# Five small edits to a hybrid scan, attention and mixture-of-experts kernel: where block 0's weights are copied, when choices are counted, and how a sigmoid is made

## The chip, the cores and the metric

The kernel runs on one core of a Trainium2 chip. The metric is the device time of one execution in microseconds (us), as the median of several runs. The engines are TensorE (PE, matmuls), VectorE (DVE), ScalarE (ACT, activation functions and copies), GpSimd (POOL) and SyncE (SP, which only starts transfers). Each engine works through its own queue of instructions in order, and semaphores make one wait for another.

## What is computed

The input is 8 sequences of 512 tokens with 256 features. Four residual blocks follow one another, each on a layernorm of its input:

```python
x = x + scan_block(layernorm(x))     # silu(x @ Win), a linear recurrence over tokens, @ Wout
x = x + mixture(layernorm(x))        # routed and shared experts
x = x + attention(layernorm(x))      # 16 heads of 16, causal, scores clipped to +-10
x = x + mixture(layernorm(x))        # the same weights again
```

The mixture is the part that the edits touch most:

```python
scores = sigmoid(x @ router_w.T)                  # 16 experts
s = scores + bias
# the best 2 of 4 groups of experts, by the sum of each group's two highest s
# then the 4 highest s within these groups
tw = 2.5 * scores[chosen] / (scores[chosen].sum() + 1e-20)
routed = sum over chosen e of tw[e] * ((silu(x @ gate[e]) * (x @ up[e])) @ down[e])
shared = (silu(x @ sh_gate) * (x @ sh_up)) @ sh_down
```

Everything is float32.

## The kernel before, in words

The work has four stages. In the profiled execution they lie at about 0 to 359 us (scan), 359 to 765 (first routed experts), 765 to 1331 (attention) and 1331 to 1758 (second routed experts and the final sums).

**The two stretches.** `stretch(layer)` (L1236) runs the scan and later the attention, one sequence ("batch", b = 0 to 7) after the other. Beside each batch's main work it carries the routing of the batch before it, the shared experts of the batch before that, and the layernorm and transposes of a batch to come. Each of these is a generator of steps, and `timed(...)` gives each step a fraction of the main work at which it is issued. The written order is then what a scheduler starts from; it may reorder instructions on each engine by its own estimates, except where `tc.issue_after` ties one behind another or `keep_in_program_order` pins it.

**Routing one batch.** `Route` (L550) normalises, transposes (`turned`, L385; `pt_m`, copies at L399), and forms logits (`pl_m`, L590). ACT turns them into `score_m` by the sigmoid of L599. A chain of some thirty VectorE operations in `choices` (L602) finds the four experts and writes `sel_m` (L649). TensorE then counts: two small matmuls `pr_m` (L656, L657) give each choice its place among all choices of its expert. VectorE makes `row_m`, `where_m`, `slots_m` from that, and GpSimd scatters the rows to memory (L706) so that each expert's rows lie together. The last batches, 6 and 7, have tighter fractions (L1329 to L1332), since the routed stage can start only when all are counted.

**Attention.** For each of four groups of heads: scores `ps_a` (L1096), exponentials on ACT (L1107) into `w_all` or `es_a`, clamping on VectorE (L1110, L1118), products with the values `po_a` (L1131), a copy `oT_a` on ACT (L1144), transposes `pto_a` (L1147), and the division by the row sums (`rec_a`, `o_a`, L1149, L1150). Then `pt_oa` and the output projection `py_a` (L454). The exponential and the sigmoid are in different tables of ACT, so ACT loads a table (ACT_TABLE_LOAD) when it goes from one to the other. The shared experts of this stretch use tanh (L972), and those of the scan use sigmoid (L976).

**Shared experts.** `shared_experts` (L943): `pg_m` matmuls of 512 columns (L958), `pd_m` matmuls (L987), a copy `ys_m` (L995). The list `wide` always holds the `pg_m` matmul made last.

**Routed experts.** `routed(i)` (L806) works on blocks of 128 sorted rows. 136 blocks are always run; an `If` (L939) holds further ones that this input does not need, so each routed stage begins behind a branch that all engines take. For block n: `load` (L833) reads the rows from memory and, for every fourth block, reads four table entries to registers (L816); `fetch` (L846) copies the block's gate weights by ACT and its up weights by VectorE from the big weight tile `w_all` to small tiles; `turn` (L854) transposes the rows on PE (`pt`, L858) and ACT copies them back (L859); `up` (L861) has 16 matmuls `ph` (L869), the sigmoid (L877) and two products; `down` (L893) has the matmuls `pyr` (L897), a scaling on ACT (L905) and an adding scatter on GpSimd (L906). Fetches run one block ahead of `up` in the written order.

**Buffers.** The small weight tiles, most routing temporaries and the scan's `xi_s` and `state_s` share one tag, "col", of 6 buffers; the scan's `y_s` and the transposed activations share "kb4", of 9. The residual stream `x` has a pool of 3 buffers of its own, `xpool`.

**The start.** `first_two` (L1277) brings batches 0 and 1 of the scan up together: layernorm of batch 0, its transposes `pt_l` with two copies to `xT_l` (L399), the input projection `pz_s` (L500), layernorm of batch 1 pinned on VectorE, the scans (L509 to L516). `layer.copies` says which engines make the two copies of a transpose: in the scan `by_scalar` (both ACT), in the attention `by_both` (ACT and VectorE).

Of the kernel before, what the change touches and what calls it, by code (L numbers as in the profile page):

```python
# [15 lines left out]
P = 128  # L16
# [58 lines left out]
def tile_hybrid_block(  # L75
# [280 lines left out]
    def timed(steps, *places):  # L356


        def scaled():
            now = 0  # L360
            for place in places:
                yield place - now
                now = place
                next(steps)
            for _ in steps:
                pass

        return Piece(1, scaled())
# [4 lines left out]
    def some(steps, many: int):  # L373

        for _ in range(many):
            yield next(steps)

    def issue(piece):
        for _ in piece.steps:
            pass  # L380
# [204 lines left out]
    def logits(i: int, b: int, tag: str, held):  # L585
        xnT = held["xnT"]
        pl = bank([P, NT, E], f"pl_{tag}")
        for t in range(NT):
            for k in range(KD):
                nc.tensor.matmul(  # L590
                    pl[:, t, :],
                    lhsT=xnT[:, k, t * P : (t + 1) * P],
                    rhs=rw_sb[:, k, :],
                    start=(k == 0),
                    stop=(k == KD - 1),
                )
            yield
        score = small.tile([P, NT, E], FP, tag="score", name=f"score_{tag}")
        nc.scalar.activation(score, pl, AF.Sigmoid)  # L599
        held["score"] = score  # L600

    def choices(i: int, b: int, tag: str, held, paced: bool):  # L602
# [50 lines left out]

        pr = bank([P, 2, NT, E], f"pr_{tag}")
        flat = sel.rearrange("p t e -> p (t e)")
        nc.tensor.matmul(pr[:, 0].rearrange("p t e -> p (t e)"), lhsT=tri, rhs=flat, start=True, stop=True)  # L656
        nc.tensor.matmul(pr[:, 1].rearrange("p t e -> p (t e)"), lhsT=ones, rhs=flat, start=True, stop=True)  # L657
        row = small.tile([P, NT + 1, E], FP, tag="row", name=f"row_{tag}", bufs=3)
        nc.vector.tensor_copy(row[:, 0, :], counts[i])
        for t in range(NT):  # L660
# [145 lines left out]
    def routed(i: int, table, beside):  # L806
# [39 lines left out]
        def fetch(n: int):  # L846


            for half, (copy, name) in enumerate(((nc.scalar.copy, "gate"), (nc.vector.tensor_copy, "up"))):
                here = work.tile([P, KD * F], FP, tag="col", name=f"{name}_{i}_{n}", bufs=COLS)  # L850
                copy(here, w_all[:, bass.ds(held[n][0] + half * KD * F, KD * F)])  # L851
                held[n].append(here)

# [382 lines left out]
    def stretch(layer):  # L1236


        i = layer.mixture
        xT, xn, made, routes, sends = {}, {}, {}, {}, []  # L1240

        def norm(b: int, first: bool = False):
            def place():
                xn[b] = kb4(f"xn_{i}_{b}")
                return xn[b]

            return normed(b, f"l{i}_{b}", place, first, first)

        def turn(b: int, copies=layer.copies):
            return turned(lambda: xn.pop(b), f"l{i}_{b}", lambda xnT: xT.update({b: xnT}), copies)  # L1250

        def project(b: int):
            made[b], piece = layer.project(b, xT.pop(b))
            return piece

        def store(b: int):
            nc.sync.dma_start(out=rows_of(parts[i][0], b), in_=x_tiles[b])

        def experts(b: int):
            return shared_experts(i, b, lambda: routes.pop(b).held["xnT"], i == 1)  # L1260

        for b in range(layer.ahead):
            if b < layer.early:
                if b in unturned:
                    issue(Piece(0, unturned.pop(b)))
                xT[b] = ready.pop(b)
            else:
                layer.load(b)
                first = i == 0 and b == 0
                issue(Piece(0, norm(b, first)))  # L1270
                issue(Piece(0, turn(b)))
                if first:
                    load_shared()
            if b == 0:
                issue(project(b))

        def first_two():  # L1277

            layer.load(1)
            issue(Piece(0, norm(1, True)))  # L1280
            for _ in range(2):
                pending.pop(0)()
            main = layer.main(0, made.pop(0))
            issue(Piece(0, some(main.steps, NI)))
            issue(Piece(0, turn(1)))
            issue(project(1))
            second = layer.main(1, made.pop(1))
            issue(Piece(0, some(second.steps, NI)))
            issue(main)
            return Piece(second.columns - NI * KD * T, second.steps)  # L1290

        def start_route(b: int):
            routes[b] = Route(i, b, layer.copies)
            store(b)
            return routes[b]

        begun = None
        if layer.mixture == 0:
            begun = first_two()
        for b in range(1 if begun else 0, B):  # L1300
            pieces = [begun or layer.main(b, made.pop(b))]
            begun = None
            nxt, last = b + layer.ahead, b == B - 1
            fill = []
            if layer.ahead > 1 and not last:
                fill.append(project(b + 1))
            if b > 1:
                shared_sum = experts(b - 2)
                if last:

                    each = shared_sum.columns // 12
                    rest = Piece((12 - HELD) * each, shared_sum.steps)

                    many = HELD * each if layer.mixture else HELD * each * 3 // 2
                    shared_sum = Piece(many, some(shared_sum.steps, HELD))
                fill.append(shared_sum)
                pieces.append(timed(sends.pop(), 0.1, 0.14, 0.18, *spread(0.22, 0.66 if last else 0.86, NT * TK)))
            if fill:
                pieces.append(behind(*fill))
            if b > 0:  # L1320
                r = start_route(b - 1)
                if last:
                    pieces.append(timed(r.norm(), *spread(0.0, 0.12, NT), *spread(*layer.last_rows, NT)))
                else:
                    first, then, rows, full = layer.norms
                    pieces.append(timed(r.norm(), *spread(first, then, NT), *spread(rows, full, NT)))
                sends.append(r.rest)
                if last:
                    pieces += [  # L1329
                        timed(r.scores(), *layer.last_scores, *spread(0.5, 0.56, NT)),  # L1330
                        timed(some(r.rest, PICKS), *spread(0.57, 0.7, PICKS)),
                        timed(some(r.rest, 3 + SENT), 0.72, 0.74, 0.76, *spread(0.78, 1.0, SENT)),  # L1332
                    ]
                else:
                    pieces += [
                        timed(r.scores(), *layer.scores[:2], *spread(*layer.scores[2:], NT)),
                        timed(some(r.rest, PICKS), *spread(*layer.choose, PICKS)),
                    ]
            if nxt < B:
                added = layer.load(nxt)  # L1340
                if added is not None:
                    pieces.append(timed(added, 0.24, 0.28))
                pieces += [
                    timed(norm(nxt), *spread(0.32, 0.44, NT), *spread(0.56, 0.64, NT)),
                    timed(turn(nxt), 0.75, 0.79),
                ]
            issue(beside(*pieces))
            if layer.ahead == 1 and nxt < B:
                issue(project(nxt))
            if i == 0 and b == 2:  # L1350
                for make in pending:
                    make()
        layer.end()

        r = start_route(B - 1)
        chain = 3 + PICKS
        issue(
            beside(  # L1360
                behind(rest, experts(B - 2)),
                timed(r.norm(by_vector=True), *spread(0.0, 0.05, 2 * NT)),
                timed(sends.pop(), *spread(0.0, 0.5, NT * TK - SENT)),
                timed(r.scores(), 0.2, 0.22, *spread(0.28, 0.33, NT)),
                timed(some(r.rest, chain + 8), *spread(0.36, 0.68, chain), *spread(0.7, 1.0, 8)),
            )
        )
        table = []
        issue(
            beside(  # L1370
                experts(B - 1),
                timed(r.rest, *spread(0.0, 0.5, NT * TK - 8)),
                timed(blocks(i, table), 0.03, 0.14, 0.26, 0.38),
            )
        )
        return table
# [140 lines left out]
```

## Time and profile before

| | |
|---|---|
| median of 3 runs | 1783.7 us (1783.02 to 1783.77) |
| the profiled execution's own time | 1759.74 us |
| its span, first to last instruction | 1758.0 us |
| PE busy | 1675.9 us, 95% |
| VectorE busy | 1100.0 us, 63% |
| ACT busy | 806.7 us, 46% |
| GpSimd busy | 769.8 us, 44% |
| mean granted TensorE clock | 0.981 of full speed |
| table loads on ACT | 17 of 1283 ns: 1 at L241, 8 at L599, 8 at L1107 |
| period of batches 2 to 5 of the attention | 69.0 us |

The profile is of one execution. A line of its list of groups or of its timeline names the engine, the line of the code, the operation, what it writes and reads, and how often; in brackets stand the idle time of the engine just before and what ended it. The ends of matmuls are modelled. TensorE's clock is granted in windows of 3.41 us, at full speed or at half.

### The profile page before, as it was taken

Reading aid. Unit: us, or ns where it says so; the run is one execution under the profiler, and the core shown is the slowest. Engines: PE = TensorE matmul, PEld = TensorE weight load, DVE = VectorE, ACT = ScalarE, POOL = GpSimd, SP = SyncE. Lnnn points to the kernel's source line nnn. Section 1 sums busy time; section 2 is a strip of 40 time slices with the busy share of each in tenths; the row PEclk is TensorE's granted clock in tenths of the full one; section 3 lists DMA queues with packets and bytes.
Section 4 is the critical chain, followed back from the end, with each engine's and each line's share of the span. In section 5 each row is a group of like instructions: output and inputs, shape, how many; then the busy total and the mean of one; then the engine's idle time right before and its main releaser. Section 6 shows DMA issues by size and latency. Waiting matters only on the chain. (4 is left out here: it accounts for less than half of the span.)

```text
span 1758.0 us, 32867 instructions
## 1 busy us (share of the span) xinstructions
PE 1675.9 (95%) x10640; PEld 1252.9 (71%) x10640; DVE 1100.0 (63%) x3428; ACT 806.7 (46%) x1740; POOL 769.8 (44%) x674
## 2 busy tenths in 40 slices
PE   6899998999999999999999999999999999999993
PEld 3566665589999999944545545545468999999993
DVE  8878877445556655556776576666653655565562
ACT  3222322145555555545654464454423555555551
POOL 3355555535555655420032331322552555455663
PEclk9999999999999999989999999999999999999997
DMA  5444323445555655531012111122543555666666
GB/s 157 139 166 161 133 91 120 163 90 94 98 94 105 108 96 97 103 63 37 25 39 70 68 61 63 52 74 68 184 148 80 98 96 94 111 128 139 119 125 170
DMA packets 149279, 181.38 MB, mean 103 GB/s; under 512 B 16144, under 2 KB 135984, under 8 KB 149104
## 3 DMA queue, kind: packets, MB, share of 16 engines
q0 software_dynamic: 54720, 82.57, 25.0%
q1 hardware_dynamic: 92576, 92.71, 17.6%
q10 hardware_dynamic: 1808, 3.93, 0.6%
q8 instruction: 89, 1.46, 0.3%
q14 instruction: 86, 0.70, 0.1%
HBM read 81.62 MB, written 97.53 MB: 102 GB/s over the span
## 5 line engine op out<-in xcount | busy, mean ns | idle before, releaser
L906 POOL DMA_INDIRECT part<-rows x272 | 426.6, 1568 | 336.8 <-ACT rows L905 244.7
L706 POOL DMA_INDIRECT xg<-sorted_m,slots_m x256 | 256.4, 1002 | 289.5 <-ACT slots_m L703 98.9
L869 PEld LDWEIGHTS ph<-rows,gate 128*128 128x128 f32 x2176 | 285.4, 192 | 21.3 <-ACT rows L859 6.7
L869 PE MATMUL ph<-rows,gate 128*128 128x128 f32 x2176 | 289.4, 276 | 5.1 <-ACT rows L859 5.1
L869 PE MATMUL ph<-rows,up 128*128 128x128 f32 x2176 | 288.7, 276 | 0.0
L897 PE MATMUL pyr<-w_all,rows 128*128 x1088 | 280.5, 380 | 0.9 <-DVE rstd_l L428 0.9
L869 PEld LDWEIGHTS ph<-rows,up 128*128 128x128 f32 x2176 | 266.2, 193 | 0.0
L877 ACT ACTIVATE rows<-ph 128x256 f32<-128x256 f32 x272 | 104.5, 384 | 329.0 <-PE ph L869 329.0
L878 DVE TENSOR_TENSOR rows<-ph,rows 128x256 f32<-128x256 f32 x272 | 115.3, 424 | 193.7 <-ACT rows L877 193.0
L897 PEld LDWEIGHTS pyr<-w_all,rows 128*128 128x128 f32 x1088 | 185.2, 191 | 15.2 <-ACT rows L905 1.3
L851 ACT COPY gate<-w_all 128x512 f32 x272 | 170.0, 626 | 15.2 <-PE ph L869 2.4
L1107 ACT ACTIVATE w_all<-ps_a 128x1024 f32<-128x1024 f32 x128 | 124.4, 1021 | 82.6 <-PE ps_a L1096 77.5
L851 DVE COPY up<-w_all 128x512 f32 x272 | 119.4, 439 | 31.7 <-PE ph L869 17.1
L905 ACT ACTIVATE rows<-pyr,gain 128x256 f32<-128x256 f32 x272 | 128.6, 473 | 15.3 <-PE pyr L897 13.7
L1096 PE MATMUL ps_a<-w_all 32*128 32x512 f32 (+3 forms) x1024 | 123.3, 477 | 7.5 <-ACT w_all L1107 6.4
L958 PE MATMUL pg_m<-xT_m,sg_sb 128*128 128x512 f32 x256 | 124.8, 610 | 0.0
L882 DVE SCALAR_TENSOR_TENSOR gain<-rows,expert_b 128x4 f32<-128x4 f32 x272 | 61.1, 225 | 100.2 <-ACT rows L905 83.5
L958 PE MATMUL pg_m<-xT_m,su_sb 128*128 128x512 f32 x256 | 123.4, 604 | 0.0
L879 DVE TENSOR_TENSOR rows<-ph,rows 128x256 f32<-128x256 f32 x272 | 115.2, 423 | 8.3
L987 PE MATMUL pd_m<-sd_sb,act_m 128*128 128x256 f32 x512 | 119.8, 382 | 0.0
L987 PEld LDWEIGHTS pd_m<-sd_sb,act_m 128*128 128x128 f32 x512 | 95.5, 190 | 20.9 <-issue 4.7
L858 PE MATMUL pt<-ident,rows 128*128 128x128 f32 x544 | 103.7, 273 | 2.9 <-PEq L816 1.0
(219 smaller groups left out, 2215.5 us busy)
## 6 DMA issues: line engine op xcount, KB each, us to landing
rows<-xg SPq DMA_DIRECT2D x272, 136.0 KB, 2.6
part<-x SPq DMA_DIRECT2D x16, 512.0 KB, 3.0
part<-ys_m SPq DMA_DIRECT2D x14, 512.0 KB, 3.0
w_all<-in_L_ffn_gate_w_dram SPq DMA_DIRECT2D x24, 256.0 KB, 5.2
w_all<-in_L_ffn_up_w_dram SPq DMA_DIRECT2D x24, 256.0 KB, 5.8
w_all<-in_L_ffn_down_w_dram SPq DMA_DIRECT2D x24, 256.0 KB, 5.7
sum<-part POOLq DMA_DIRECT2D x10, 512.0 KB, 4.0
xg<-zeros SPq DMA_DIRECT2D x34, 136.0 KB, 2.2
```

The costliest lines, as they stand in the source:

```text
L706: nc.gpsimd.indirect_dma_start(out=xg[i], out_offset=bass.IndirectOffsetOnAxis(ap=slots[:, at : at + 1], axis=0), in_=rows[:, t, :], in_of ...
L851: copy(here, w_all[:, bass.ds(held[n][0] + half * KD * F, KD * F)])
L869: nc.tensor.matmul(ph[:, s, f * P : (f + 1) * P], lhsT=both[s][:, k * F + f * P : k * F + (f + 1) * P], rhs=rows[:, ROW + k * P : ROW + (k ...
L878: nc.vector.tensor_mul(act, ph[:, 0, :], act)
L879: nc.vector.tensor_mul(act, ph[:, 1, :], act)
L897: nc.tensor.matmul(py, lhsT=act[:, f * P : (f + 1) * P], rhs=w_all[:, bass.ds(w + 2 * KD * F + f * D, D)], start=(f == 0), stop=(f == KF - 1),
L905: nc.scalar.mul(rows[:, 0:D], py, gain[:, TK : TK + 1])
L906: nc.gpsimd.indirect_dma_start(out=parts[i][n % 2], out_offset=bass.IndirectOffsetOnAxis(ap=rows[:, D + 2 * TK : D + 2 * TK + 1].bitcast(U ...
L958: made = nc.tensor.matmul(dst, lhsT=w[:, k, f * P : (f + 1) * P], rhs=xnT[:, k, :], start=(k == 0), stop=(k == KD - 1),)
L987: nc.tensor.matmul(py[:, j, :], lhsT=acts[n][:, f, t * P : (t + 1) * P], rhs=shared[n][3][:, f, :], start=(n == 0 and f == 0), stop=(n == ...
L1096: nc.tensor.matmul(ps[j // 2][:, j % 2, col : col + n], lhsT=k_sb[w][r, o, c * P : (c + 1) * P], rhs=q_sb[r, o, c * P : T], start=True, st ...
L1107: nc.scalar.activation(es[two], ps[two][:, :, 0:cols], AF.Exp, scale=ATT_SCALE)
```

## The change

There are five edits.

1. The router's score in the second mixture (the one beside the attention) is made by exp(-x) on ACT, then on VectorE min with 3e38, plus 1, and a reciprocal. The first mixture keeps the sigmoid.
2. In batch 6 of both stretches the two counting matmuls `pr_m` are tied behind the `pg_m` matmul that was issued last.
3. In each routed stage block 0's gate and up are both copied by VectorE, into the two halves of one tile `both` from `xpool`, instead of by ACT and VectorE into two "col" tiles.
4. The first transpose of the scan (batch 0) is copied by ACT and VectorE, instead of twice by ACT.
5. In the last batch of each stretch, the last step of the choices and the sends of the batch before it stand at later fractions.

```diff
--- before.py
+++ after.py
@@ -596,7 +596,13 @@
                 )
             yield
         score = small.tile([P, NT, E], FP, tag="score", name=f"score_{tag}")
-        nc.scalar.activation(score, pl, AF.Sigmoid)
+        if i == 0:
+            nc.scalar.activation(score, pl, AF.Sigmoid)
+        else:
+
+            nc.scalar.activation(score, pl, AF.Exp, scale=-1.0)
+            nc.vector.tensor_scalar(score, score, 3.0e38, 1.0, ALU.min, ALU.add)
+            nc.vector.reciprocal(score, score)
         held["score"] = score
 
     def choices(i: int, b: int, tag: str, held, paced: bool):
@@ -653,8 +659,9 @@
 
         pr = bank([P, 2, NT, E], f"pr_{tag}")
         flat = sel.rearrange("p t e -> p (t e)")
-        nc.tensor.matmul(pr[:, 0].rearrange("p t e -> p (t e)"), lhsT=tri, rhs=flat, start=True, stop=True)
-        nc.tensor.matmul(pr[:, 1].rearrange("p t e -> p (t e)"), lhsT=ones, rhs=flat, start=True, stop=True)
+        with tc.issue_after(wide[-1].ins) if b == B - 2 else nullcontext():
+            nc.tensor.matmul(pr[:, 0].rearrange("p t e -> p (t e)"), lhsT=tri, rhs=flat, start=True, stop=True)
+            nc.tensor.matmul(pr[:, 1].rearrange("p t e -> p (t e)"), lhsT=ones, rhs=flat, start=True, stop=True)
         row = small.tile([P, NT + 1, E], FP, tag="row", name=f"row_{tag}", bufs=3)
         nc.vector.tensor_copy(row[:, 0, :], counts[i])
         for t in range(NT):
@@ -846,8 +853,15 @@
         def fetch(n: int):
 
 
+            if n == 0:
+
+                both = xpool.tile([P, NT, D], FP, tag="x", name=f"both_{i}").rearrange("p t d -> p (t d)")
             for half, (copy, name) in enumerate(((nc.scalar.copy, "gate"), (nc.vector.tensor_copy, "up"))):
-                here = work.tile([P, KD * F], FP, tag="col", name=f"{name}_{i}_{n}", bufs=COLS)
+                if n == 0:
+                    here = both[:, half * KD * F : (half + 1) * KD * F]
+                    copy = nc.vector.tensor_copy
+                else:
+                    here = work.tile([P, KD * F], FP, tag="col", name=f"{name}_{i}_{n}", bufs=COLS)
                 copy(here, w_all[:, bass.ds(held[n][0] + half * KD * F, KD * F)])
                 held[n].append(here)
 
@@ -1268,7 +1282,7 @@
                 layer.load(b)
                 first = i == 0 and b == 0
                 issue(Piece(0, norm(b, first)))
-                issue(Piece(0, turn(b)))
+                issue(Piece(0, turn(b, by_both if first else layer.copies)))
                 if first:
                     load_shared()
             if b == 0:
@@ -1328,8 +1342,8 @@
                 if last:
                     pieces += [
                         timed(r.scores(), *layer.last_scores, *spread(0.5, 0.56, NT)),
-                        timed(some(r.rest, PICKS), *spread(0.57, 0.7, PICKS)),
-                        timed(some(r.rest, 3 + SENT), 0.72, 0.74, 0.76, *spread(0.78, 1.0, SENT)),
+                        timed(some(r.rest, PICKS), *spread(0.57, 0.67, PICKS - 1), 0.76),
+                        timed(some(r.rest, 3 + SENT), 0.79, 0.81, 0.83, *spread(0.85, 1.0, SENT)),
                     ]
                 else:
                     pieces += [
```

In the built order of instructions, edit 3 puts the two VectorE copies of block 0, and the first register loads of L816 on PE, ACT and VectorE, ahead of the branch at L939. Edit 1 leaves four executed table loads: at L241, one at the first L1107, and past the branch of the second routed stage one at L851, before block 1's gate copy, and one at L877, before block 0's sigmoid. Edits 2 and 5 change no order in the first stretch. In the second, batch 6's `pr_m` moves behind `pto_a` and the 24 `po_a` matmuls that read `w_all`, ahead of the eight that read `es_a`; on VectorE the clamps of the last two `es_a` come ahead of `sel_m`, and `rec_a` and `o_a` of the third group directly after it. Edit 4 moves VectorE's half of the copy ahead of the layernorm of batch 1; the first scan operations then stand between that layernorm's steps, and on ACT the `xT_l` copies of batch 1 come after an activation `xi_s` that takes over an earlier `xi_s` buffer, free only once `y_s` has been made from it.

## The prediction

> **What bounds the kernel now.** I read the summary of busy times first, then a table of busy time by stage, then the waits of TensorE (PE), then the timeline around each long one.
>
> ```profile
> PE 1675.9 (95%) x10640; PEld 1252.9 (71%) x10640; DVE 1100.0 (63%) x3428; ACT 806.7 (46%) x1740; POOL 769.8 (44%) x674
> ```
>
> PE is busy 95% of the span of 1758.0 us. So only PE's gaps, and windows in which its clock is halved, can be won or lost. The table by stage (stretch, its length, PE busy, VectorE, ScalarE, GpSimd, granted clock):
>
> ```profile
> 1050.00:1119.00 69.00, 68.92 (x432) 35.38 (x428) 46.03 (x145) 34.55 (x57) 19.84 (x21) 1.00 0.18 64
> 1240.00:1290.00 50.00, 45.77 (x267) 27.46 (x260) 33.72 (x126) 19.16 (x39) 26.02 (x27) 0.97 0.51 171
> ```
>
> The first is one ordinary batch of the attention: PE is full, although ScalarE (ACT) makes two table loads in it. The second holds batch 6, the place that the edits aim at: 4.2 us of PE are idle. The list of PE's waits says for what:
>
> ```profile
> PE pr_m L656 <- DVE sel_m L649: 7.1, 3, 3.2
> PE pz_s L500 <- ACT xT_l L399: 7.0, 1, 7.0
> PE ps_a L1096 <- ACT w_all L1107: 6.4, 13, 1.0
> PE ph L869 <- ACT rows L859: 5.1, 4, 2.3
> ```
>
> These are the three counting waits (batch 6 twice, batch 7 once), one at the start, the small ones on exponentials, and the first blocks of the two routed stages. The timeline of batch 6 and of the second routed stage's start:
>
> ```profile
> 1248.77 1.28 ACT L599 ACT_TABLE_LOAD   x1
> 1250.39 1.28 ACT L1107 ACT_TABLE_LOAD   x1
> ...
> 1257.93 0.43 PE L656 MATMUL pr_m<-sel_m,tri 128*128 128x64 f32 x2 [2.99 <-DVE sel_m L649]
> 1258.50 1.06 PE L1147 MATMUL pto_a<-ident,oT_a 128*128 128x128 f32 x4
> 1263.10 1.98 PE L958 MATMUL pg_m<-xT_m,su_sb 128*128 128x512 f32 x4
> 1266.58 0.30 PE L397 MATMUL pt_oa<-ident,o_a 128*128 128x128 f32 x1 [0.62 <-DVE o_a L1150]
> ...
> 1332.19 1.66 ACT L851 COPY gate<-w_all 128x512 f32 x3 [1.22 <-DMA rows<-xg]
> 1333.76 0.64 ACT L859 COPY rows<-pt 128x256 f32<-128x256 f32 x2
> 1334.17 2.07 PE L869 MATMUL ph<-rows,gate 128*128 128x128 f32 x8 [2.24 <-ACT rows L859]
> ```
>
> Batch 6 stalls 2.99 us for sel_m, and the four transposes after it take 1.06 us where four take 0.60 later: the clock record at 1258.34 is a 3.41 us window at half speed. At the second boundary PE waits 2.24 us while ACT copies three gates of 0.52 us ahead of block 0's rows.
>
> **What the Trainium skill says.** "TensorE: Matmul & The Clock Gate", Part 1, What's actually happening: an idle window of 3413 ns halves the clock, and windows run free of the kernel. The trace agrees in length and speed (every slow record is 3.41 us or a multiple at 0.5), and in freedom: a 3.2 us stall at 292.7 brought two slow windows, the similar idle at 359 to 362 none. "ScalarE: Activation LUTs", What ACT_TABLE_LOAD costs, has 1283 ns and a drain of about 1380 ns. All 17 loads here take 1283 ns; no drain shows: after the load at 1282.71 the activation starts at 1284.00. I take 1.28. "ScalarE activation tables: per-element evaluation and per-set limits", Table sets in the compiler and the runtime, says that loads are placed per block. That fits what the built order of the changed kernel shows: past the branch into the second routed stage ACT has two new loads, one before block 1's gate copy, one before block 0's sigmoid.
>
> **The change, part by part**, against the profiled execution (span 1758.0, time 1759.74). The shown median, 1783.7, is 24.0 longer; I carry differences over unchanged.
>
> *Sigmoid from exp in the second mixture.* It removes 15 loads (all at the scores, and seven of eight at L1107) and adds the two named: net 13 x 1.283 = 16.7 us of ACT. Against that PE gains little. In batches 2 to 5 PE has 68.92 of 69.00: 0, hidden by PE's own matmuls, and with that cover gone it would be worth the 2.6 us per batch. In batch 1 two waits of 0.38 and 0.21 follow the loads at 851.2 and 853.3: -0.6. Two VectorE operations on 128x64 come per batch: no row has these exact ones; between 128x64 operations at 0.23 and a 128x16 reciprocal at 0.26, I take 0.45 for both, bounded by 0.3 and 0.7. They lie in VectorE's slack (46 of 69) except in batch 7, where pr_m already waits 0.87 on sel_m at 1293.30: the load's absence gives back 0.2 there (the last logits end at 1283.76, the score starts at 1284.00), so +0.25.
>
> *Counting later, batch 6.* In the first mixture PE's order is unchanged: 0, and the 3.21 us stall with its two slow windows stays. In the second, pr_m now stands behind the four transposes pto_a and 24 of the 32 po_a matmuls, ahead of the last eight. On VectorE the two pairs of es clamps go ahead of sel_m. Replay: without loads the score is there before VectorE ends its clamps at 1249.6; plus 0.35 s_m starts at 1249.95 (now 1250.32). From s_m to the end of sel_m now takes 7.48 (to 1257.80, next start); with the es clamps, 1.07 (1257.80 to 1258.87), sel_m ends at 1258.5. PE: the ps_a group at 1252.79 takes 0.64 instead of 1.52, because its exponentials come 2.6 earlier; po_a 0.57, so 1254.0. oT is copied from 1254.3 to 1254.9, pto_a ends at 1255.4, 24 po_a at full clock (about 2.1) at 1257.5. A stall of 1.1 remains. Then pr 0.57, po_a 0.55: pg_m starts at 1259.7 instead of 1263.10, pto_a ends at 1262.0. What is late next is o_a, since the row, found and choices operations wait behind the later pr_m: from 1259.2 they need 2.3, then sig 0.6, rec 0.3, act 0.7, o_a ends at 1263.6, and pt_oa follows at 1263.7 against 1266.58: -2.9. A slow window in the remaining stall would give back up to 1.7 (half of 3.41). I take -2.5; bounds -6 (stall, slow window and ps_a waits, all gone: 2.99+0.38+1.7+0.9) and -0.8.
>
> *Block 0's gate and up by VectorE.* The two copies and the register load of the table (L816) move ahead of the branch; VectorE idles 7 us there, so they are hidden, and without it they would cost about 1.1. After the branch ACT still has three gate copies (blocks 1, 2, 3) before rows_0, so the 1.66 us stay; the register load of 0.31 and 0.07 of register work leave: -0.4 at each boundary. At the second the new load stands ahead of the gates: +1.28. The load at the sigmoid falls in ACT's 3.59 us of idle: 0. Blocks 1 to 13 are reordered slightly on each engine; the stages show 401.5 of 405 and 245.5 of 246 us PE busy: 0, within 0.5.
>
> *The first turn by ACT and VectorE.* The second half of xT is copied by VectorE (0.69), ahead of norm(1), and the first scan operations come between. ACT's xT copies of batch 1, on which PE waits 6.95 us to 28.80, now stand behind an activation that waits until y_s has been made and a buffer is free: about 28.6 instead of 28.18. +0.4; bounds -1.0 (batch 0 starts 0.3 earlier, and the clock with it) and +2.5 (norm(1) late by 2.2).
>
> *Later fractions.* No queue but batch 6's changes: 0. GpSimd's order moves one memset, SyncE's queue nothing, so no DMA is issued later: 0.
>
> Sum: -0.6 + 0.25 - 2.5 - 0.4 - 0.4 + 1.28 + 0.4 = -2.0. Time 1757.7 profiled, 1781.7 median.
>
> **The rivals.**
> (a) The counting stall goes wholly, with its slow window, and a window at a boundary is lost as well: -6 + 0.5, or to -8 with a window less. For it: the remaining stall is only 1.1, which VectorE's pipelining may cover. Against: VectorE's queue before sel_m is longer. About 1777.8.
> (b) Slower: the new table load at the second boundary. There PE already idles 0.92 and 2.24 us and meets two slow windows; 0.9 net more idle shifts everything, and the first boundary, with no slow window today, can get one or two by mere phase. One window costs up to 1.7; it decides when two more are met, 3.4, plus 0.9 and a start at its bound of +2.5, against -2.5: +4, 1788. The start's slow windows at 26 and 50 speak for it; that the windows' place is chance speaks against a large chance.
> (c) The loads are on the path after all: -16.7, 1767. Against it is PE's 68.92 of 69.00.
> (d) The moves cancel: the later o_a eats batch 6's gain: 0 to +3, 1785.
>
> **How the numbers follow.** A measurement of this kernel tells about 0.2%, 3.6 us, from no change. The worked case has 0.44, a tenth of all beyond -3.6; (a) 0.28, (b) 0.19, (c) 0.02, (d) 0.07. Faster: 0.10 + 0.28 + 0.02 = 0.40; same: 0.34 + 0.07 = 0.41; slower 0.19. The range runs from 1776.3, where (a) is mostly in, to 1787.8, where most of (b) is; outside are about 0.06 below and 0.12 above. The worked case alone spans 1779 to 1783.5.
>
> **What would show it.** Right: loads fall from 17 to 4; ordinary batches stay 69.0; pr_m in batch 6 waits about 1.1 us, and the next pg_m starts about 3.4 us sooner counted from the batch's pl_m; at the second boundary ph waits about 3.1 us, with a load among the gates; at the first about 1.9; pz_s of batch 1 starts near 29. Wrong: batches below 68.5 us (c); pr_m's wait gone and the clock whole (a); more half-speed windows before 1700 us than the twelve of now, or pz_s after 31 (b). The forecast fails most easily on slow windows, which no order of instructions tells.

## The result and the profile after

The changed kernel takes 1776.7 us (median of 20 runs, 1768.6 to 1781.5), the kernel before in the same comparison 1783.8 (20 runs, 1778.3 to 1789.2). The ratio is 0.9951, with a 95% interval from 0.9938 to 0.9963: 7 us less by the medians, 9 by the ratio, where 2.0 were forecast. The median lies just inside the range given (its lower end is 1776.3); by the ratio the time would be 1775.0, just outside, and the change is about four times the size forecast.

The profile shown for before is of an execution of 1759.74 us, 24 below the median, with a span of 1758.0; that of after is of an ordinary run, with a span of 1777.8. Set side by side, the two say "20 us slower". So the first thing to find out was what the 24 us are.

From the page of after, its first line and TensorE's busy time:

```profile
span 1777.8 us, 32866 instructions
PE 1686.0 (95%) x10640; PEld 1258.2 (71%) x10640; DVE 1100.0 (62%) x3447; ACT 787.9 (44%) x1724; POOL 770.7 (43%) x674
```

ScalarE is busy for 787.9 us instead of 806.7: 13 of the 17 table loads are gone. The stages table shows what that bought in an ordinary batch of the attention (stretch, its length, PE, weight loads, VectorE, ScalarE, GpSimd, clock, share and GB/s of the DMAs; the prediction's tables have the same columns, and its list of them leaves out the weight loads):

```profile
1056.00:1125.00 69.00, 68.91 (x432) 35.39 (x428) 46.58 (x148) 31.97 (x54) 20.00 (x20) 1.00 0.19 64
```

Nothing: 68.91 of 69.0 us, as before, with 2.6 us less on ScalarE. The waits of PE in after, from the third row on (the work that waits and what releases it, then the sum in us, the number and the longest; the lines of after are numbered up to 14 higher):

```profile
PE ph L883 <- ACT rows L873: 5.8, 4, 3.1
PE pg_m L972 <- ACT expert_b L793: 5.1, 1, 5.1
PE ps_a L1110 <- ACT w_all L1121: 5.0, 10, 1.0
PE pr_m L663 <- DVE mv_m L413: 5.0, 1, 5.0
PE pr_m L663 <- DVE sel_m L655: 4.5, 1, 4.5
PE pz_s L500 <- ACT xT_l L399: 2.6, 1, 2.6
```

Two waits of about 5 us and one of 4.5 are new beside the profile shown of before (the 5.0 is the scan's batch 6, which had 3.2; the 4.5 its batch 7). At the start pz_s waits 2.6 us instead of 7.0, but most of that has only moved: the transposes pt_l there now wait four times instead of once, 12.7 us instead of 9.8. The attention's batch 6 is no longer in the list. The second boundary, in the timeline of after:

```profile
1346.89 0.66 PE L872 MATMUL pt<-ident,rows 128*128 128x128 f32 x4 [0.92 <-ACTq L953]
1347.42 1.28 ACT L865 ACT_TABLE_LOAD   x1 [0.83 <-DVE gain L896]
1348.71 1.66 ACT L865 COPY gate<-w_all 128x512 f32 x3
1350.69 3.78 PE L883 MATMUL ph<-rows,both 128*128 128x128 f32 x16 [3.15 <-ACT rows L873]
1350.93 1.28 ACT L891 ACT_TABLE_LOAD   x1
```

The new load stands ahead of the gates and PE waits 3.15 us instead of 2.24; the second load is hidden. That is as forecast.

### The profile page after: what moved, and what is told of

Its sections match the earlier page's. It is cut to its first block, busy times and chain, and to the rows that moved or that the text cites. A ratio compares the mean times of both kernels' runs of the same rounds, so it can differ in the third digit from the quotient of the medians.

```text
span 1777.8 us, 32866 instructions
## 1 busy us (share of the span) xinstructions
PE 1686.0 (95%) x10640; PEld 1258.2 (71%) x10640; DVE 1100.0 (62%) x3447; ACT 787.9 (44%) x1724; POOL 770.7 (43%) x674
## 5 line engine op out<-in xcount | busy, mean ns | idle before, releaser
L972 PE MATMUL pg_m<-xT_m,su_sb 128*128 128x512 f32 x256 | 127.8, 622 | 5.1 <-ACT expert_b L793 5.1
```

Of the source, the lines that this page charges most:

```text
L972: made = nc.tensor.matmul(dst, lhsT=w[:, k, f * P : (f + 1) * P], rhs=xnT[:, k, :], start=(k == 0), stop=(k == KD - 1),)
```

## The experiments

Each study ran on one chip, with the kernel before among its runs. Ratios are to that kernel, with 95% intervals. Two kinds of trace turned up, and all kernels of a study were of one kind: in one kind (the profile shown of before) the kernel before takes about 1762 us, in the other 1784 to 1795. The result above and the first, third and last studies are of the second kind, here called "late"; the other two are "prompt". The exp score, alone or with all five edits, was run only where signals are late.

| kernel | kind | ratio to before |
|---|---|---|
| the kernel before, unchanged | late | 1.0000 (0.9988 to 1.0011) |
| all five edits | late | 0.9964 (0.9952 to 0.9977), again 0.9949 (0.9925 to 0.9972) |
| score only | late | 1.0008 (0.9993 to 1.0022) |
| all but the score | late | 0.9936 (0.9917 to 0.9955), again 0.9945 (0.9927 to 0.9964) |
| first copy only | prompt | 0.9992 (0.9979 to 1.0005) |
| first copy only | late | 0.9947 (0.9922 to 0.9972) |
| later counting only | prompt | 0.9966 (0.9947 to 0.9985) |
| later counting only | late | 0.9982 (0.9964 to 1.0000) |
| block 0's copies only | prompt | 0.9990 (0.9978 to 1.0001) |
| start shifted | prompt | 0.9996 (0.9983 to 1.0009), again 1.0003 (0.9988 to 1.0018) |
| first copy, start shifted | prompt | 1.0002 (0.9990 to 1.0015) |
| first copy, start shifted | late | 1.0003 (0.9988 to 1.0019) |
| sends spread | prompt | 0.9993 (0.9981 to 1.0005) |
| sends spread | late | 1.0002 (0.9989 to 1.0016) |
| first copy and later counting | prompt | 0.9943 (0.9921 to 0.9965) |

**First study: which half.** No edit, for the first:

> The kernel before, unchanged, for its trace and for the scatter of the comparison. Every theory: ratio 1.000 within 0.002. Its span should be near the median's, about 1782, not the 1758 of the profile shown; the 24 us between them should be seen as places where the waits of TensorE are longer or its clock is halved more often. If the two profiles agree everywhere and only the tail differs, the 24 us are outside the edits' reach.

> All five edits, for a second trace and as the yardstick of this chip. Every theory: 5 to 9 us faster than before (measured so far: ratio 0.9951). If the waits of 4.5 us at 326 and 5.1 us at 1331 in the profile after belong to the changed order, they are here again at the same places; if they are chance, they are elsewhere or gone.

The score alone is this on the kernel before, and "all but the score" is the change without it:

```diff
-        nc.scalar.activation(score, pl, AF.Sigmoid)
+        if i == 0:
+            nc.scalar.activation(score, pl, AF.Sigmoid)
+        else:
+            nc.scalar.activation(score, pl, AF.Exp, scale=-1.0)
+            nc.vector.tensor_scalar(score, score, 3.0e38, 1.0, ALU.min, ALU.add)
+            nc.vector.reciprocal(score, score)
```

> Only the score in the second mixture from exp; the counting, the copies and the fractions as before. Theory 'loads' (the absent table loads are worth more in a usual execution than in the one profiled): 4 to 7 us faster. Theory 'order' (the gain is in where counting, copies and transposes stand): within 2 us of before, since the ordinary batches had TensorE busy 68.92 of 69.0 us.

> The four other edits with the sigmoid and its 16 table loads left as before. Theory 'loads': 0 to 3 us faster. Theory 'order': 5 to 8 us faster. Should both this and the score alone give about half, the gains add and neither theory holds alone.

The score alone is not faster (1.0008), and the other four edits give 0.9936. "Loads" falls; "order" stands, with 11 us where it expected 5 to 8. The new trace of before also shows where the 24 us come from; each computing engine's instructions stand in it in the same order as in the profile shown. Its longest wait, in the list of PE's waits:

```profile
PE pr_m L656 <- DVE sel_m L649: 17.5, 3, 13.6
```

In the profile shown it was 3.2. The timeline around it (PE, then VectorE, then PE):

```profile
286.60 3.62 PE L454 MATMUL py_s<-w_scan,y_s 128*128 128x256 f32 x16
301.25 0.69 DVE L463 TENSOR_TENSOR x<-py_s,x 128x512 f32<-128x512 f32 x1 [10.30 <-remote]
303.82 0.69 PE L656 MATMUL pr_m<-sel_m,tri 128*128 128x64 f32 x2 [13.60 <-DVE sel_m L649]
```

The py_s matmuls end at 290.2 by the record. The addition that reads them starts at 301.25, on an idle VectorE; the trace has PE's semaphore update at 301.22. Behind that addition in VectorE's queue stands the rest of the choice of experts, behind that sel_m, and PE itself waits for sel_m. In the profile shown the same update comes at 289.5, at once. The same thing happens after the block table's small matmuls, at the end of both stretches, 4.9 to 7.1 us late in all late traces but one (later counting only: at once in the first stretch, 3.0 in the second); in the prompt ones ScalarE's copy starts 0.04 us after them. In the new trace of before:

```profile
1335.59 1.25 PE L782 MATMUL pe_b<-chosen_b,cand_e 128*128 128x143 f32 x8
1343.64 0.28 ACT L786 COPY expert_b<-pe_b 128x143 f32<-128x143 f32 x1 [10.98 <-remote]
1343.97 2.93 PE L958 MATMUL pg_m<-xT_m,su_sb 128*128 128x512 f32 x3 [5.09 <-ACT expert_b L786]
```

pe_b is done at 1336.8, and ACT's copy starts 6.8 us later. So after's wait of 5.1 us for expert_b is no work of the edits; before has it too. Its 5.0 in the scan's batch 6 stands where before has 13.6. The 4.5 in batch 7 before has not (0.00 there): it is in all six late traces with the first copy on VectorE and the start unshifted, at 1.6 to 4.6 us.

**Second study: single edits** (it came out prompt).

```diff
-                issue(Piece(0, turn(b)))
+                issue(Piece(0, turn(b, by_both if first else layer.copies)))
```

> Only the first transpose's second copy on VectorE. The four edits without the score gave 0.9936, and their trace differs from that of before most in two places: TensorE's wait at the start (8.7 us before, 2.5 and 2.7 after) and the counting wait of batch 6 of the scan stretch (13.6 us before, 4.9 after), where none of the edits changes any order. Theory 'start' (this copy makes the start shorter, and all later places come earlier, the counting wait included): this alone 5 to 9 us faster, and pr_m of batch 6 waits about 5 us. Theory 'counting' (the gain is in the attention's batch 6 and in the boundaries): within 2 us of before, with the wait of 13 us still there.

```diff
+        with tc.issue_after(wide[-1].ins) if b == B - 2 else nullcontext():
             ...  # the two pr matmuls
-                        timed(some(r.rest, PICKS), *spread(0.57, 0.7, PICKS)),
-                        timed(some(r.rest, 3 + SENT), 0.72, 0.74, 0.76, *spread(0.78, 1.0, SENT)),
+                        timed(some(r.rest, PICKS), *spread(0.57, 0.67, PICKS - 1), 0.76),
+                        timed(some(r.rest, 3 + SENT), 0.79, 0.81, 0.83, *spread(0.85, 1.0, SENT)),
```

> Only the later counting and the later fractions. Theory 'counting': 3 to 6 us faster, with pr_m's wait of 3.0 us in the attention's batch 6 down to 1 or less. Theory 'start': 1 to 3 us faster for the same trace, and the wait of 13 us in the scan's batch 6 unchanged.

```diff
+            if n == 0:
+                both = xpool.tile([P, NT, D], FP, tag="x", name=f"both_{i}").rearrange("p t d -> p (t d)")
...
+                if n == 0:
+                    here = both[:, half * KD * F : (half + 1) * KD * F]
+                    copy = nc.vector.tensor_copy
```

> Only block 0's gate and up by VectorE. By the sum of the prediction 0.4 us at each boundary: within 1.5 us of before under both theories. More than 3 us faster would mean that the boundary of the routed stages is where the gain lies, and both theories fall.

```diff
+                if first:
+                    for t in range(NT):
+                        same = x_tiles[b][:, t, :]
+                        tc.keep_in_program_order(nc.vector.tensor_copy(same, same))
                 issue(Piece(0, norm(b, first)))
```

> The kernel before, with four copies of the first input tile onto itself on VectorE ahead of the first layernorm, so that everything starts about 1 us later in nearly the same order. Theory 'start': about 1 us slower, the wait of 13 us in batch 6 unchanged. Theory 'phase' (that wait is long or short by how the moment falls against the scatters running beside it, and an earlier start merely moved it): the wait changes by several us, and the time with it.

The wait of 13 us is not in this study's traces, so its first and last kernel decide nothing on it. Where signals are prompt, only the later counting counts alone: 0.9966, some 6 us with an interval of 3 to 9. Its trace, PE's timeline in the attention's batch 6, against that of block 0's copies alone, which has the old counting:

```profile
1254.56 0.43 PE L656 MATMUL pr_m<-sel_m,tri 128*128 128x64 f32 x2 [3.00 <-DVE sel_m L649]
1255.09 1.06 PE L1154 MATMUL pto_a<-ident,oT_a 128*128 128x128 f32 x4
```

```profile
1256.36 0.41 PE L657 MATMUL pr_m<-sel_m,tri 128*128 128x64 f32 x2 [0.68 <-DVE sel_m L649]
1261.32 0.66 PE L397 MATMUL pt_oa<-ident,o_a 128*128 128x128 f32 x4 [0.98 <-DVE o_a L1151]
```

The stall falls from 3.0 to 0.68 us, and with it the half-speed window that made the four transposes take 1.06. From the start of the batch's last logits matmul to the second group of pt_oa it takes 16.74 us here, and 19.5 to 21.4 in the seven prompt traces with the old counting (19.5 with a window of 3.4 us at half speed, 21.0 and more with two).

**Third study: the same where signals are late, and the sum.**

> All five edits once more, beside single ones on one chip. Two kinds of trace have been seen: in one (the profile shown of before; the kernel before takes about 1762) the signals of TensorE reach other engines at once, in the other (before at 1784 to 1788) some come up to 11 us late. Theory 'counting' (the later counting brings the gain by itself): as fast as the later counting alone, 5 to 7 us faster than before, whichever kind comes. Theory 'late signals' (most of the gain exists only where signals are late): 7 to 9 us faster in the second kind, 2 to 3 in the first.

> The four edits without the score. Theory 'the score costs' (two more VectorE operations and a table load at the second boundary): 2 to 4 us faster than all five. Theory 'the score is free': equal to all five within 1.5 us, and the 5 us between them in the first comparison was scatter.

> The first transpose's copy alone. Where signals are late: if the long counting wait in the scan's batch 6 (13.6 us before) shrinks by the earlier start alone, 5 to 8 us faster; if not, within 1.5 us. Where they are not: within 1.5 us, as measured (0.9992).

> The later counting and fractions alone. Measured where signals are not late: 0.9966. Theory 'counting': the same 4 to 8 us again in either kind, with pr_m's wait in the attention's batch 6 under 1 us instead of 3.0.

Here the first copy alone gives 0.9947, as much as all five edits (0.9949), and the later counting 0.9982, less than "counting" expected: "late signals" stands. The timeline of the first copy alone shows where; no computing engine's order differs from that of before after the first 82 us:

```profile
285.27 3.62 PE L454 MATMUL py_s<-w_scan,y_s 128*128 128x256 f32 x16
291.37 0.69 DVE L463 TENSOR_TENSOR x<-py_s,x 128x512 f32<-128x512 f32 x1 [1.75 <-remote]
293.94 0.69 PE L656 MATMUL pr_m<-sel_m,tri 128*128 128x64 f32 x2 [5.05 <-DVE mv_m L413]
```

The addition comes 2.5 us after the matmuls instead of 11, and the counting waits 5.05 us instead of 13.60 (the wait is put down to mv_m, but sel_m, which the counting reads, ends at 293.89). Part of it is given back up to the first routed block: from this counting to there the trace takes 77.7 us, that of before 75.1, and the shifted one below 72.8. In this kind of trace every kernel of the first and third study that has the first copy, and after too, has the short wait, 4.9 to 5.1 us; those without it have 12.2 to 13.8. Whether the score costs time in sum stays open: all five and all but the score differ by 0.0004 in this study, by 0.0028 in the first, where the intervals barely overlap.

**Fourth and fifth: the moment, or the order?**

The kernels: the shift again; the shift together with the first copy; the first copy with the later counting; and the sends of batch 6 of each stretch, beside the last batch, at other fractions:

```diff
-                pieces.append(timed(sends.pop(), 0.1, 0.14, 0.18, *spread(0.22, 0.66 if last else 0.86, NT * TK)))
+                pieces.append(timed(sends.pop(), 0.1, 0.14, 0.18, *spread(0.22, 0.86, NT * TK)))
```

> The kernel before with four copies of the first input tile onto itself ahead of the first layernorm, about 1 us later in nearly the same order. If signals are late on this chip: theory 'moment' (the 11 us late signal before the counting of the scan's batch 6 is long or short by the moment at which it falls) expects that wait to change from 13.6 us by more than 3; theory 'order' (something in the early order that the first transpose's copy changes) expects it at 12 to 14 us and the time 0 to 2 us slower. If signals are not late here, no difference, as before (0.9996).

> The first transpose's copy on VectorE together with the same four copies, so that its earlier start is mostly taken back. Where signals are late: theory 'moment' expects the counting wait of batch 6 back at 10 to 14 us and the gain of 9 us gone; theory 'order' expects the wait at 5 us and 7 to 9 us faster than before still.

> The kernel before, with the sends beside the last batch at the fractions that the other batches use (up to 0.86 instead of 0.66), so that the scatters do not run back to back while the counting waits. Theory 'train' (signals of TensorE are held while scatters run back to back, and come when the train stops): the wait of 13.6 us falls below 7 where signals are late, and the kernel is 3 to 8 us faster there. If the wait stays, the train is not the reason. Where signals are not late: within 2 us.

> The first copy and the later counting together, without the score and block 0's copies. If single gains add (0.9947 and 0.9982 where signals are late, 0.9992 and 0.9966 where not): 0.993 and 0.996, as fast as the four edits without the score (0.9945 and 0.9936); then block 0's copies bring nothing.

That study came out prompt, so three of its four questions were not put; shift and spread make no difference there. The first copy with the later counting gives 0.9943, 10 us (6 to 14), by its median of 1752.2 us the shortest time of all. Two questions were put once more, and this time signals were late:

> The first transpose's copy with the four extra copies ahead of it. Where signals are late: theory 'moment' expects the counting wait of the scan's batch 6 at 10 to 14 us and the time equal to before within 2 us; theory 'order' expects the wait at 5 us and 7 to 9 us faster than before. Where they are not late: equal to before (measured 1.0002).

> The kernel before with the sends beside the last batch spread up to 0.86. Where signals are late: theory 'train' expects the wait of 13.6 us below 7 and 3 to 8 us faster; if the wait stays at 12 to 14, the scatters' back-to-back train as such does not hold the signal. Where they are not late: equal to before within 2 us (measured 0.9993).

The first copy with the later start (2.3 us at the first pz_s, 0.7 at the matmuls below) has lost its whole gain: 1.0003. Its wait:

```profile
285.97 3.62 PE L454 MATMUL py_s<-w_scan,y_s 128*128 128x256 f32 x16
300.68 0.69 DVE L463 TENSOR_TENSOR x<-py_s,x 128x512 f32<-128x512 f32 x1 [9.91 <-remote]
303.25 0.69 PE L656 MATMUL pr_m<-sel_m,tri 128*128 128x64 f32 x2 [13.66 <-DVE sel_m L649]
```

The late signal is back, 11.1 us after the matmuls, though the kernel still has the edit. In this trace and in that of the first copy alone every computing engine's instructions stand in the same order, but for the four extra copies at 3.7 us. So it is not the edit's order that shortens this wait but the moment it brings about; "order" falls. What the moment is measured against stays open. It is not the time since the start: with the sends spread, the same matmuls end at 288.7 us, nearly as in the first copy alone (288.9), and the signal is 11 us late all the same. Nor is it the place between two scatters: in 19 of the 20 traces, prompt and late, these matmuls end 1.19 to 1.21 us after a scatter's start by the record, whether the signal comes at once, 2.4 us or 11 us later. Nor did that run decide on the scatters, since it did not open their train: they still followed each other every 1.26 us up to 296.3. What the late traces agree in is that some held signals come when such a train ends (its last start at 297.87 and PE's update at 301.22 in the new trace of before; 1340.47 and 1343.62 at its second boundary), but the signal at 291.4 above comes in mid-train. A train's end can also follow from the late signal, since the slots of the next scatters come from VectorE, which waits for it.

## Why the prediction was wrong, step by step

*"I carry differences over unchanged"* is the step that failed. The working noted that the median is 24.0 us above the profiled execution and did not ask why. The median belongs to executions in which PE's signals come late at some places, the profile to one in which they don't. A wait of 3.2 us in the profile is 13.6 in the runs that are timed, and it was priced as unchanged. It is not all: where signals are prompt, as in the profile, the first copy and the later counting gained 10 us (6 to 14), and their terms were +0.4 and -2.5. The traces there show 2.7 us in the attention's batch 6 and 0.7 at the start; where the rest lies was not found.

*The first turn: +0.4, bounds -1.0 and +2.5.* The start itself was within the bounds with the wrong sign: pz_s of batch 1 begins at 27.9 to 28.2 us in every trace of the edit without the shift, against 28.8 in the profile shown, so -0.7 (the other unshifted traces without the edit have 29.1 to 30.3). But where signals are late the edit is worth 9.5 us (5 to 14), far outside the bounds, and most of what the traces show of it arises at the counting of the scan's batch 6. This is the largest term of the measured 7 to 9 us, nothing in the profile shown could have told it, and it is luck: a start a little later takes it away.

*Counting later: -2.5, bounds -6 and -0.8.* The mechanism was right and the size near: the remaining stall 0.68 us where 1.1 were worked out, pt_oa 2.8 us earlier than in the traces with one half-speed window where 2.9 were. By time it is 6 us where prompt (3 to 9), 3 where late (0 to 6). What the replay had wrong is whose gain it is: it counted on the absent table loads, but 16.74 us are reached with the loads in place. With the score from exp and the later counting the same stretch takes 18.2 to 19.5 us in three traces, all late; late ones with the sigmoid take 16.75 to 17.5. The counting starts 13.3 to 14.4 us after the logits instead of 11.8 to 12.5. So in batch 6 the score costs 0.8 to 2.8 us there, not nothing. Two things can be read. VectorE's two operations take 0.20 and 0.55 us, 0.75 together, where 0.45 was taken and 0.7 was the upper bound; so s_m starts as late as with the load (1256.15 against 1256.12 in the traces of all five edits and of all but the score). And ScalarE, without loads, now waits for TensorE. With all five edits:

```profile
1254.00 1.69 PE L1110 MATMUL ps_a<-w_all 32*128 32x128 f32 x16
1258.61 1.94 ACT L1121 ACTIVATE w_all<-ps_a 128x1024 f32<-128x1024 f32 x2 [3.92 <-issue]
1259.66 0.69 DVE L1124 SCALAR_TENSOR_TENSOR w_all<-w_all,causal 128x512 f32<-128x512 f32 x1 [1.59 <-ACT w_all L1121]
```

With all but the score, where ps_a ends at the same moment within 0.1 us:

```profile
1256.19 1.28 ACT L1115 ACT_TABLE_LOAD   x1
1257.48 1.94 ACT L1115 ACTIVATE w_all<-ps_a 128x1024 f32<-128x1024 f32 x2
```

The matmuls ps_a end at 1255.69 by the record, and their signal comes at 1258.5: in three of the four traces with the exp score it is 2.8 to 2.9 us late here. So the exponentials start 1.1 us later without the load than behind it, and VectorE, ahead of sel_m, waits for them. What the score does in batch 6 where signals are prompt no run shows.

*Sigmoid from exp.* Hidden in the ordinary batches, as forecast (68.91 of 69.00); +1.28 at the second boundary as forecast (the wait of ph is 3.52 us in the trace of the score alone, 2.24 before); in batch 7 s_m starts 1.37 us after the last logits instead of 0.76, +0.6 where +0.25 was forecast; in sum nothing gained where signals are late (1.0008). Rival (c), all loads on the path, would have shown here and does not.

*Block 0's gate and up: -0.4 at each boundary.* In the one trace of it alone, from pr_m of batch 7 to the first ph, the two boundaries take 40.4 and 40.5 us, against 40.9 and 40.8 to 40.9 in the prompt traces without it: -0.5 and -0.4. By time 0.9990, with an interval (0.9978 to 1.0001) that just includes no change.

*The rivals.* (a), the stall gone with its window, came nearest in time (1777.8), and half of it happened: the stall is nearly gone, and the window with it in all five traces of the later counting with the sigmoid (two of the three with the exp score still have one). But the 7 us are mostly another wait. (b) happened in its mechanism, a longer wait at the second boundary, and in its sign: after has two half-speed windows at each boundary and 19 before 1700 us, where twelve were counted. But the late trace of before has 21, so they need not be the edits' work. (d) did not happen: the second pt_oa is not later.

## What to carry to other kernels

Where the profiled execution and the median differ by more than the change is likely to be worth, find out first which waits differ; a profile of an ordinary run is worth more than a careful sum on an extraordinary one. A gain that appears far from the edit, where no order has changed, can hang on a moment: shift the start by a microsecond and see whether it stays. Moving a small consumer of a long VectorE chain behind work that is ready (here the counting behind 28 matmuls) was worth most of its stall and the half-speed window after it, by the traces in both kinds of run; by time it is clear only where signals are prompt.

## What the runs showed of the hardware

Signals of TensorE to other engines came at once in some executions, and in others up to 11.2 us after the modelled end of the matmul, in the places looked at always after groups of short matmuls beside GpSimd's scatters (py_s, the block table, the last transposes, ps_a in batch 6), and then often several within 0.4 us. In the late executions the trace also holds fewer semaphore updates: 42 to 71 of DMAs from 280 to 300 us where the prompt ones have 240 to 256, and 1392 from TensorE where the same kernel has 1777 in the prompt trace. Whether the signal is held up or the matmul's end is later than modelled, and why whole studies are of one kind, no run here shows. It is not the chip alone: the second and the third study ran on one and the same chip, the one prompt, the other late.

The kernel before takes 22 to 33 us more in these executions (1784 to 1795 for 1762). Its two traces differ by 34.5 us: 10.4 are the wait in the scan's batch 6 (13.6 for 3.2), 4.2 come from there to the counting of batch 7, 1.2 at the first boundary, 7.3 at the second, where the block table's signal is late, 6.4 behind it, and the other 5.0 are spread over the rest.
